# First images of the second layer: the turned block is made by VectorE in 32x32 pieces, and the transform along w runs as 64x64 tiles over four quarters of w

## The chip, the cores and the metric

The kernel runs on one core of one Trainium2 chip. The metric is the device time of one execution in microseconds (us). Three runs of the kernel before gave 2610.23, 2604.98 and 2619.08 us; their median is 2610.23 us. A difference of about 0.5% (13 us) is what a measurement of this kernel can tell from no change.

Engine names follow the profile: PE is the matmul engine (its weight loads are PEld), DVE is VectorE, ACT is ScalarE, POOL is GpSimd, SP is the engine that only issues DMAs.

## The reference, cut to what matters

The input is an image `x` of 256 x 256 pixels with 128 channels, in float32. Layer 0 is gated attention with two biases over each row. Layer 1 reads the result as 256 "tokens" (the first image axis), each an image of H = 256 rows by W = 128 pixels (the second axis by the channels), and runs a small Fourier neural operator over them. Its last part is a pair of mixing layers over groups of four tokens:

```python
h0 = instance_norm(attn, norm2_w, norm2_b)
h1 = fno_layer(h0, mix_wr[0], mix_wi[0], ..., (H, W), norm=True, act=True)
h2 = fno_layer(h1, mix_wr[1], mix_wi[1], ..., (H, W), norm=True)
out = instance_norm(h2, mon_w, mon_b) + attn

def fno_layer(x, wr, wi, bias, sw, sb, out_hw, norm=False, act=False):
    skip = jnp.einsum('bihw,oi->bohw', x, sw) + sb[:, None, None]
    xf = spectral_conv(x, wr, wi, bias, out_hw)      # FFT, 32 x 16 modes mixed, inverse FFT
    if norm: xf = instance_norm(xf)
    y = xf + skip
    return jax.nn.gelu(y, approximate=False) if act else y
```

What is changed lies between `h1` and the second layer's spectrum: `h1` is made block by block, and each block is at once transformed along w to 16 complex frequencies (32 real rows), the first half of the second layer's FFT.

## The kernel before, in words

The 256 tokens are worked on in two halves of 128, called a = 0 and a = 1, with one token on each partition. The stage in question is `first_images(a, ...)` (line 1719). It goes over 16 blocks b of a half; a block `hb[b]` holds 16 image rows by 128 pixels for all 128 tokens, 2048 numbers on each partition. Image rows are taken by their remainder j modulo 4 (`by_turn`); for row class j the four groups of 32 tokens stand in another order on the partitions (group i at i XOR j), because `skip` (line 1396) writes group i to partitions 32*(i^j).

The order of the work on PE, ACT, DVE and POOL is that of the program text (`manual_schedule`); SP's DMA issues are in program order too. Engines wait for each other only where data or buffers ask for it. One pass of the loop, at index b, issues in this order:

- `load(b+1)` and, for a = 0, `load_w(b+1)`: DMAs on SP for the modes `gs` and for `y2` (a = 1) or the old image `xw` (a = 0).
- `first_skip(b)` (16 matmuls of 32x32 into four PSUM banks `ups`) and `second_skip(b-2)` (16 more into four banks `sps`, then four `bn_stats` on DVE). For a = 1 the second one stands ahead of the first.
- `image(b)` (line 1386): 16 matmuls of 32x128 that add the inverse transform along w into the same four `ups` banks.
- `gelu` of row classes 0 and 1 on ACT (line 1821), from the `ups` banks into `hb[b]`.
- `along_w(b-2)` (line 1799): four matmuls with 128 contraction rows and 32 output rows, 512 columns each, into one bank `psA`; one ACT copy to `yA` (line 1806); one DMA to DRAM, `Yd`, on POOL's queue (line 1807). Its place in ACT's order is between the two pairs of `gelu`.
- `gelu` of row classes 2 and 3.
- `turn_back(b-1)` (line 1769): 16 PE transposes of 128x128 through four PSUM banks `htps`, and four copies to `hT` (line 1788 on DVE; row class 0 by line 1779, on DVE for a = 0 and on ACT for a = 1). The reversed views in these copies put the tokens back into their order.
- For a = 0 `add_w(b+1)` (line 1746): ACT scales (line 1754), POOL adds (line 1757) and issues the DMA to the output (line 1758), for those half blocks that were not done earlier.

The `sps`, `psA` and `htps` banks come from one ring of four; `ups` from another ring of four. For a = 1 the pass is followed by a step of `output_0`, which makes the final output of half 0: 16 matmuls and an `image` into banks `h2ps` of the `ups` ring, evacuated by ACT (line 2141) and DVE (line 2139), then two accumulating DMAs on POOL's queue (line 2163). `Yd` is read back by `second_modes` (a = 0, line 1892) and by `LastModes` (a = 1, lines 1972 and 1977), which transform along h.

Of the kernel before, what the change touches and what calls it, by code (L numbers as in the profile page):

```python
# [10 lines left out]
FP = mybir.dt.float32  # L11
# [7 lines left out]
P = 128  # L19
# [681 lines left out]
def layer1(tc, I, C, ident, x1d, upool, U, Q2, groups, out):  # L701
# [6 lines left out]
    nc = tc.nc  # L708
    NT, H, W = 256, 256, 128
    L = lambda n: I["L1_conv_" + n]  # L710
    with ExitStack() as ctx:
# [667 lines left out]
        def by_turn(t):  # L1379

            return t.rearrange("p (n j w) -> p j n w", j=4, w=W)

        def rows_of(ps):
            return ps.rearrange("p (n w) -> p n w", w=W)

# [51 lines left out]

        sp = sp3
        hstat = sp.tile([P, 64, 6], FP, name="hstat")
        ystat = sp.tile([P, 2, 64, 6], FP, name="ystat")  # L1440
        with tc.tile_pool(name="psb", bufs=4, space=PSUM) as psa:

            ps = psa.tile([P, 512], FP, tag="a", name="chps")
# [44 lines left out]
        for a in range(2):  # L1488
            h = Half()
            halves.append(h)  # L1490
            h.col = sp.tile([P, 16], FP, name=f"col_{a}")
            h.turn = sp.tile([P, 8], FP, name=f"turn_{a}")
            h.bl0 = sp.tile([P, P], FP, name=f"bl0_{a}")
            h.sums, h.summed = False, set()
            h.Gd1 = dram.tile([32, 4, 64, P], FP, name=f"Gd1_{a}")
            h.Gd2 = dram.tile([32, 4, 64, P], FP, name=f"Gd2_{a}")
            h.Yd = dram.tile([H, 32, P], FP, name=f"Yd_{a}")

        def y_blocks(a, psum, lo, hi, also=None):

            tt = slice(a * P, (a + 1) * P)
            gs = {}

            def load(u):
                if (a, u) not in xts:
                    xts[a, u] = load_x1(a, u)
                if u % 2 == 0:
                    gs[u // 2] = xp.tile([P, 4, P], FP, tag="gs", name=f"gs_{a}_{u}", bufs=3)
                    load_modes(gs[u // 2], Gd0, u // 2, tt)

            load(lo)
            load(lo + 1)
            yield 0.0
            for u in range(lo, hi):
                b, s = u // 2, u % 2
                if u + 2 < hi:
                    load(u + 2)
                xt = xts.pop((a, u))
                ps = [psum.pool.tile([P, 512], FP, tag=psum.tag, name=f"yps_{a}_{u}_{j}") for j in range(4)]
                ps = [z[:, 0:256] for z in ps]  # L1520
                for j in range(4):
                    for sc in range(2):
                        nc.tensor.matmul(  # L1523
                            rows_of(ps[j]), mpT[:, sc, tt], by_turn(xt[:, sc])[:, j],
                            start=(sc == 0), stop=False,
                        )
                    if j < 3:
                        yield 0.86
                image(ps, gs[b], bsy, range(2 * s, 2 * s + 2))
                if a == 0:  # L1530
                    yt = blocks[:, b, s * HB : (s + 1) * HB]
                else:
                    yt = xp.tile([P, HB], FP, tag="yt", name=f"yt_{u}")
                for j in range(4):
                    nc.vector.tensor_tensor(by_turn(yt)[:, j], rows_of(ps[j]), bc(rwb, 1, 2), ALU.mult)  # L1535
                for g in range(2):
                    nc.vector.bn_stats(ystat[:, a, 2 * u + g, :], yt[:, g * 512 : (g + 1) * 512])
                if a:
                    nc.gpsimd.dma_start(ydv[:, a, u * HB : (u + 1) * HB], yt)  # L1539
                if also:  # L1540
                    also(u, xt)
                yield 1.62
# [99 lines left out]
        def first_modes(a, wp, mk, psum, gts):  # L1642
# [6 lines left out]
            )  # L1649
            dg = mk("m", [P, 2, P], f"dg3_{a}")  # L1650
            ym, yv, ra, lam, r2, rho, sig = (h.col[:, k : k + 1] for k in range(7))
            nc.vector.bn_aggr(h.col[:, 0:2], ystat[:, a].rearrange("p k s -> p (k s)"))
            yield 1.0
            rsqrt(nc, wp, ra, yv, EPS, "rq")
            nc.vector.tensor_mul(lam, ra, an[:, 0:1])
# [63 lines left out]
        def first_images(a, wp, yp, psk, pst, first=None, modes=()):  # L1719
# [44 lines left out]
            if a == 0:  # L1764
                load_w(0)
                add_w(0)
            hTs = {}

            def turn_back(b):

                turned = by_turn(hb[b])
                hT = hTs[b] = {}
                for j in (1, 2, 3, 0):
                    ps = pst.tile(f"htps_{a}_{b}_{j}")
                    for n in range(4):
                        nc.tensor.transpose(ps[:, n * P : (n + 1) * P], turned[:, j, n, :], ident)  # L1776
                    t = hT[j] = wp.tile([P, 512], FP, tag="hT", name=f"hT_{a}_{b}_{j}", bufs=4)
                    if j == 0:
                        (nc.scalar.copy if a else nc.vector.tensor_copy)(t, ps)
                        continue  # L1780
                    v = t.rearrange("p (n c d x) -> p n c d x", n=4, c=2, d=2)
                    if j == 1:
                        v = v[:, :, :, ::-1].rearrange("p n c d x -> p (n c) d x")
                    elif j == 2:
                        v = t.rearrange("p (n c x) -> p n c x", n=4, c=2)[:, :, ::-1]
                    else:
                        v = t.rearrange("p (n c x) -> p n c x", n=4, c=4)[:, :, ::-1]
                    nc.vector.tensor_copy(
                        v, ps.rearrange("p (m c x) -> p m c x", m=v.shape[1], c=v.shape[2])
                    )  # L1790

            def second_skip(b):

# [4 lines left out]

            def along_w(b):

                hT = hTs.pop(b)
                psA = pst.tile(f"psA_{a}_{b}")
                for j in (1, 2, 3, 0):
                    nc.tensor.matmul(psA[32 * j : 32 * j + 32, :], bfwd, hT[j], start=True, stop=True)  # L1804
                yA = wp.tile([P, 512], FP, tag="yA", name=f"yA_{a}_{b}")
                nc.scalar.copy(yA, psA)
                (nc.scalar if a and b == 15 else nc.gpsimd).dma_start(
                    h.Yd[16 * b : 16 * b + 16].rearrange("(n j) f t -> (j f) n t", j=4),
                    yA.rearrange("f (n t) -> f n t", n=4),
                )  # L1810

            def first_skip(b):
# [68 lines left out]
        def second_modes(a, wp, mk, psum, gts, yts):  # L1881
# [5 lines left out]
            def load(c, hcs=(0, 1)):  # L1887
                yp, tag, bufs = yts[c]
                if c not in YT:
                    YT[c] = yp.tile([P, 2, 2, 512], FP, tag=tag, name=f"YT_{a}_{c}", bufs=bufs)  # L1890
                for hc in hcs:
                    nc.sync.dma_start(
                        YT[c][:, hc],
                        h.Yd[P * hc : P * hc + P].rearrange("h (r f) t -> h r (f t)", r=2)[
                            :, :, 4 * c * P : 4 * (c + 1) * P
                        ],
                    )

            def forward(c):
                ps = psum.tile(f"f1ps_{a}_{c}")  # L1900
                for r in range(2):
                    for hc in range(2):
                        for k in range(2):
                            for f in range(4):
                                nc.tensor.matmul(
                                    ps[32 * f : 32 * f + 32, r * P : (r + 1) * P],
                                    efwd[:, hc, (2 if r else 1) if k else 0, :],
                                    YT[c][:, hc, 1 - r if k else r, f * P : (f + 1) * P],
                                    start=(hc == 0 and k == 0), stop=(hc == 1 and k == 1),
                                )  # L1910
                nc.vector.tensor_copy(F[:, c].rearrange("p r t -> p (r t)"), ps[:, 0:256])
# [48 lines left out]
        class LastModes:  # L1960
# [5 lines left out]
            def load(self):  # L1966

                tile = lambda tag, bufs, n, name: xp.tile([P, 2, n], FP, tag=tag, name=name, bufs=bufs)
                rows = halves[1].Yd.rearrange("h (r f) t -> h r (f t)", r=2)
                self.low = [tile("xt", 3, 1024, f"YT0_{k}") for k in range(2)]  # L1970
                for k in range(2):
                    nc.sync.dma_start(self.low[k], rows[0:P, :, 1024 * k : 1024 * k + 1024])
                self.high = [tile("yt", 2, 512, f"YT1_{k}") for k in range(2)] + [tile("xt", 3, 1024, "YT1_2")]
                at = (slice(0, 512), slice(512, 1024), slice(1024, 2048))
                for lo, hi in ((0, 96), (96, P)):
                    for t, c in zip(self.high, at):
                        nc.sync.dma_start(t[lo:hi], rows[P + lo : P + hi, :, c])

            def spectrum(self, c, hc, r, f):
                if hc == 0:  # L1980
                    t, c = self.low[c // 2], c % 2
                else:
                    t, c = self.high[min(c, 2)], c % 2 if c > 1 else 0
                return t[:, r, 512 * c + f * P : 512 * c + (f + 1) * P]

            def synth(self, c, banks, gt, engines):

# [304 lines left out]
def constants():  # L2292
    H, W = 256, 128
    N = H * W
# [89 lines left out]
    c["efwd"] = trig.reshape(3, 32, 2, 128).transpose(3, 2, 0, 1)  # L2384
    tw = 2 * np.pi * np.outer(np.arange(16), w) / W
    bw = np.stack([np.cos(tw), -np.sin(tw)])
    c["bfwd"] = bw.reshape(32, W).T / N
    bs = bw * np.where(np.arange(16) == 0, 1, 2)[None, :, None]
    c["bsyn"] = np.tile(bs.reshape(32, W), (4, 1))
    c["atmean"] = np.where(np.arange(128) % 32 == 16, -1, 0)[:, None]  # L2390
# [63 lines left out]
```

## Time and profile before

| what | value |
|---|---|
| median of three runs | 2610.23 us |
| the profiled execution | 2606.34 us, span 2604.6 us |
| mean granted PE clock | 0.955 of full |
| busy over the span | PE 92%, PEld 60%, DVE 77%, ACT 54%, POOL 57% |
| first PE instruction on `psA`, half 0 and half 1 | 1969.9 and 2262.1 us |
| last one of half 1 | 2405.4 us |
| PE transposes `htps` | 512 instructions, 273 ns each (median) |
| PE matmuls `psA` | 256 instructions, 617 ns each (median) |
| DMA `Yd` on POOL's queue | 31 of 256 KB, 7.4 us from issue to landing (median) |

Every float32 matmul is two instructions in the trace; a PE transpose is one. Times on PE overlap: tiles in different corners of the array run side by side, so the busy time of a group is shorter than its count times its mean. Layer 0's attention scores alone (line 395) run until 1417 us. The stage of this change runs from about 1956 to 2087 us for half 0 and from about 2240 to 2409 us for half 1.

### The profile page before, as it was taken

The numbers are of one execution on the slowest core, as the hardware profiler recorded it, in microseconds if no ns is written. First come the engines' busy times: TensorE is split into PE (matmuls) and PEld (weight loads), VectorE is DVE, ScalarE is ACT, GpSimd is POOL, SyncE is SP. The second block draws the span as 40 slices with busy tenths as digits, with TensorE's granted clock in tenths as the row PEclk, the third lists the DMA queues.
The fourth block names the chain that finished last, engine by engine and source line by source line (L and its number), as shares of the span: only waits on it lengthen the run. The fifth ranks groups of instructions, "written<-read, shape, count | busy, mean of one in ns | idle before, by whom it ended". The sixth has DMA issues, their size and how long they took to land. (4 is left out here: it accounts for less than half of the span.)

```text
span 2604.6 us, 88676 instructions
## 1 busy us (share of the span) xinstructions
PE 2395.0 (92%) x37598; PEld 1555.3 (60%) x37598; DVE 2013.6 (77%) x2876; ACT 1399.0 (54%) x2700; POOL 1485.0 (57%) x1043
## 2 busy tenths in 40 slices
PE   7899999999999999999999899998989988899754
PEld 6555655656566556565655567787665565555633
DVE  7799999999999999999999457566655645355455
ACT  0377888888888888888887222000015501344232
POOL 1299999999999999999998003001136512221011
PEclk9999999999999999999999999999999998899855
DMA  9755565656566566565663110887897773899699
GB/s 367 219 100 104 103 107 104 105 106 108 103 107 106 102 108 106 104 108 103 108 105 72 25 59 11 266 274 260 309 336 253 268 251 112 228 285 254 205 388 343
DMA packets 1014245, 441.71 MB, mean 170 GB/s; under 512 B 830806, under 2 KB 946473, under 8 KB 1009496
## 3 DMA queue, kind: packets, MB, share of 16 engines
q1 hardware_dynamic: 977816, 347.93, 53.8%
q0 software_dynamic: 22832, 81.54, 9.8%
q10 hardware_dynamic: 13200, 6.56, 0.9%
q8 instruction: 298, 4.88, 0.8%
q14 instruction: 99, 0.81, 0.1%
HBM read 300.59 MB, written 135.27 MB: 167 GB/s over the span
## 5 line engine op out<-in xcount | busy, mean ns | idle before, releaser
L422 POOL TENSOR_TENSOR e<-e,b1T 128x1024 f32<-128x1024 f32 x255 | 604.4, 2370 | 84.5 <-ACT e L404 83.9
L427 POOL TENSOR_TENSOR es<-e 128x512 f32<-128x512 f32 x512 | 647.4, 1286 | 0.1
L449 DVE RECIPROCAL av<-av 128x256 f32<-128x256 f32 x256 | 452.2, 1766 | 9.1
L404 ACT ACTIVATE sc<-sc,b2T 128x512 f32<-128x512 f32 x514 | 340.0, 662 | 122.5 <-PE sc L395 109.9
L404 ACT ACTIVATE e<-sc,b2T 128x512 f32<-128x512 f32 x510 | 323.4, 694 | 0.0
L420 DVE TENSOR_TENSOR e<-sc,b1T 128x1024 f32<-128x1024 f32 x257 | 312.2, 1215 | 7.0 <-ACT sc L404 3.6
L395 PE MATMUL sc<-qkT 32*128 32x256 f32 x4096 | 294.8, 401 | 1.2 <-DVE e L420 1.2
L437 PE MATMUL av<-e,v 128*32 128x256 f32 x4096 | 268.7, 379 | 1.8 <-DVE gate L450 1.7
L1523 PE MATMUL yps<-xt,mpT 128*128 128x256 f32 x1024 | 246.3, 391 | 25.6 <-DVE yt L1535 12.8
L395 PEld LDWEIGHTS sc<-qkT 32*128 32x128 f32 x4096 | 185.7, 184 | 113.4 <-issue 52.7
L1523 PEld LDWEIGHTS yps<-xt,mpT 128*128 128x128 f32 x1024 | 191.6, 193 | 70.8 <-DVE yt L1535 22.9
L437 PEld LDWEIGHTS av<-e,v 128*32 128x32 f32 x4096 | 130.1, 109 | 125.9 <-issue 38.5
L1539 POOL DMA_DIRECT2D yd<-yt x32 | 17.4, 545 | 319.2 <-DVE yt L1535 319.2
L367 ACT ACTIVATE qkT<-qk,qb 128x512 f32<-128x512 f32 x256 | 174.4, 681 | 3.2 <-PE qk L337 3.0
L337 PE MATMUL qk<-turned,wT_wk 128*32 128x256 f32 x2048 | 164.5, 393 | 0.4 <-DVE g_ve L35 0.4
L494 ACT ACTIVATE turned<-turned 128x256 f32<-128x256 f32 x256 | 104.4, 408 | 111.7 <-DVE x1b L462 109.3
L337 PEld LDWEIGHTS u<-adft,x 128*32 128x32 f32 x4096 | 118.5, 110 | 74.9 <-issue 74.7
L442 PE MATMUL av<-es,ones 128*32 128x256 f32 x2048 | 160.7, 379 | 1.6 <-POOL es L427 1.6
L345 DVE STREAM_TRANSPOSE turned<-xk 128x1024 f32<-128x1024 f32 x128 | 157.9, 1234 | 0.4 <-DMA xk<-in_L_conv_kv_x_dram 0.2
L337 PE MATMUL qk<-turned,wn_wq 128*32 128x256 f32 x2048 | 157.9, 380 | 0.0
L1821 ACT ACTIVATE blocks<-ups,turn 128x512 f32<-128x512 f32 x128 | 92.7, 783 | 107.5 <-PE ups L1391 107.5
L337 PE MATMUL u<-adft,x 128*32 128x129 f32 x4096 | 137.0, 273 | 0.0
(577 smaller groups left out, 4146.7 us busy)
## 6 DMA issues: line engine op xcount, KB each, us to landing
xt<-x1d SPq DMA_DIRECT2D x128, 512.0 KB, 6.1
U<-in_x_dram SPq DMA_DIRECT2D x32, 1024.0 KB, 10.3
xk<-in_x_dram SPq DMA_DIRECT2D x512, 64.0 KB, 3.2
xk<-in_L_conv_kv_x_dram SPq DMA_DIRECT2D x512, 64.0 KB, 2.7
x1d<-x1b SPq DMA_DIRECT2D x512, 64.0 KB, 2.2
out_dram<-w POOLq DMA_DIRECT2D x64, 512.0 KB, 7.2
x<-x1d SPq DMA_DIRECT2D x126, 256.0 KB, 3.3
y<-yd SPq DMA_DIRECT2D x62, 512.0 KB, 8.8
```

The costliest lines, as they stand in the source:

```text
L337: nc.tensor.matmul(out[hd], w[:, hd], src, start=start, stop=stop)
L345: nc.vector.transpose(turned[:, a : b + 1 : b - a].rearrange("p k (b c) -> p k b c", c=32), t)
L367: nc.scalar.activation(r["qkT"], ps, AF.Identity, bias=self.qb)
L395: nc.tensor.matmul(sc[h // 2][:, h % 2, c * 256 : (c + 1) * 256], qkT[p, 256 + c * P : 256 + (c + 1) * P], qkT[p, 0:256], start=True, stop ...
L404: nc.scalar.activation(r["e"][1][:, :, c, :] if hp and s < NS - 1 else z, z, AF.Exp, bias=b2T[:, c, s : s + 1])
L420: nc.vector.tensor_tensor(e, sc.rearrange("p h x -> p (h x)"), w, ALU.mult)
L422: nc.gpsimd.tensor_tensor(e, e, w, ALU.mult)
L427: nc.gpsimd.tensor_tensor(es, e[:, :, 0, :], e[:, :, 1, :], ALU.add)
L437: nc.tensor.matmul(ps[hd, 0:256], p["v"][:, 2 * (s % 2) + c, hd], r["e"][h // 2][:, h % 2, c, :], start=(c == 0), stop=(c == 1),)
L442: nc.tensor.matmul(ps[32 * h : 32 * h + 32, 256:512], self.ones, r["es"][h // 2][:, h % 2, :], start=True, stop=True,)
L449: nc.vector.reciprocal(rd, rd)
L1523: nc.tensor.matmul(rows_of(ps[j]), mpT[:, sc, tt], by_turn(xt[:, sc])[:, j], start=(sc == 0), stop=False,)
```

## The change

`turn_back` no longer uses PE and PSUM. Two DVE transposes per block, each of 1024 numbers on each partition, turn every 32x32 piece in place of the 128x128 transposes. After them a partition holds one pixel of a quarter of w for a group of 32 tokens, so `along_w` has to add up four quarters of w, and it does so for two token groups at once: 16 matmuls of 64 contraction rows, 64 output rows and 256 columns, in four tiles of 64x64, four in a row added up in each tile. Half of each weight block is zero; its non-zero places (g XOR j) put the token groups back into order. The result lies in two banks, is copied by two ACT instructions of 256 columns each, and goes to DRAM in another layout, in runs of 64 numbers where there were runs of 128. The readers of `Yd` follow that layout. `turn_back`'s buffer is one tile of 2048 numbers in place of four of 512. `ystat` is shared by the two halves, and the constant `bfwd` grows from 128 x 32 to 128 x 512 numbers. The loop's order of calls is as before; with the PE transposes gone, `along_w` is the last work on PE in a pass.

```diff
-        ystat = sp.tile([P, 2, 64, 6], FP, name="ystat")
+        ystat = sp.tile([P, 64, 6], FP, name="ystat")
...
-            h.Yd = dram.tile([H, 32, P], FP, name=f"Yd_{a}")
+            h.Yd = dram.tile([H, 2, 2, 16, 64], FP, name=f"Yd_{a}")
...
-            hTs = {}
+            turned = {}
 
             def turn_back(b):
 
-                turned = by_turn(hb[b])
-                hT = hTs[b] = {}
-                for j in (1, 2, 3, 0):
-                    ps = pst.tile(f"htps_{a}_{b}_{j}")
-                    for n in range(4):
-                        nc.tensor.transpose(ps[:, n * P : (n + 1) * P], turned[:, j, n, :], ident)
-                    t = hT[j] = wp.tile([P, 512], FP, tag="hT", name=f"hT_{a}_{b}_{j}", bufs=4)
-                    if j == 0:
-                        (nc.scalar.copy if a else nc.vector.tensor_copy)(t, ps)
-                        continue
...
-                    nc.vector.tensor_copy(
-                        v, ps.rearrange("p (m c x) -> p m c x", m=v.shape[1], c=v.shape[2])
-                    )
+                T = turned[b] = wp.tile([P, 8, 8, 32], FP, tag="hT", name=f"hT_{a}_{b}", bufs=1)
+                src = hb[b].rearrange("p (n k l x) -> p k n l x", k=2, l=8, x=32)
+                for k in range(2):
+                    nc.vector.transpose(T[:, :, k::2].rearrange("p l n x -> p n l x"), src[:, k])
...
             def along_w(b):
 
-                hT = hTs.pop(b)
-                psA = pst.tile(f"psA_{a}_{b}")
-                for j in (1, 2, 3, 0):
-                    nc.tensor.matmul(psA[32 * j : 32 * j + 32, :], bfwd, hT[j], start=True, stop=True)
-                yA = wp.tile([P, 512], FP, tag="yA", name=f"yA_{a}_{b}")
-                nc.scalar.copy(yA, psA)
+                T = turned.pop(b)
+                ps = [pst.tile(f"psA_{a}_{b}_{r}") for r in range(2)]
+                for c in range(4):
+                    for j in range(2):
+                        for r in range(2):
+                            q, o = slice(64 * r, 64 * r + 64), slice(64 * j, 64 * j + 64)
+                            nc.tensor.matmul(
+                                ps[r][o, 0:256], bfwd[q, j, c], T[q, 4 * j + c],
+                                start=(c == 0), stop=(c == 3),
+                            )
+                yA = wp.tile([P, 4, 4, 32], FP, tag="yA", name=f"yA_{a}_{b}")
+                for r in range(2):
+                    nc.scalar.copy(
+                        yA[:, :, 1:3] if r else yA[:, :, 0::3],
+                        ps[r][:, 0:256].rearrange("p (n k x) -> p n k x", k=2, x=32),
+                    )
                 (nc.scalar if a and b == 15 else nc.gpsimd).dma_start(
-                    h.Yd[16 * b : 16 * b + 16].rearrange("(n j) f t -> (j f) n t", j=4),
-                    yA.rearrange("f (n t) -> f n t", n=4),
+                    h.Yd.rearrange("(k l) r g f x -> (l r g f) k x", l=2)[:, 8 * b : 8 * b + 8],
+                    yA.rearrange("p n (k h) x -> p (n k) (h x)", k=2),
                 )
...
+        def by_token(t):
+
+            return t.rearrange("p (g f h x) -> p f h g x", g=2, h=2, x=32)
...
                     nc.sync.dma_start(
-                        YT[c][:, hc],
-                        h.Yd[P * hc : P * hc + P].rearrange("h (r f) t -> h r (f t)", r=2)[
-                            :, :, 4 * c * P : 4 * (c + 1) * P
-                        ],
+                        YT[c][:, hc].rearrange("p r (g f x) -> p r g f x", g=2, x=64),
+                        h.Yd[P * hc : P * hc + P, :, :, 4 * c : 4 * c + 4],
                     )
...
-                                    YT[c][:, hc, 1 - r if k else r, f * P : (f + 1) * P],
+                                    by_token(YT[c][:, hc, 1 - r if k else r])[:, f],
...
-    c["bfwd"] = bw.reshape(32, W).T / N
+    fw = np.zeros((2, 2, 32, 2, 4, 2, 2, 16))
+    for g in range(2):
+        for j in range(2):
+            fw[:, g, :, j, :, :, g ^ j] = (bw.reshape(2, 16, 4, 32) / N).transpose(3, 2, 0, 1)
+    c["bfwd"] = fw.reshape(128, 2, 4, 64)
```

More of the change, by code (lines that the diff above doesn't have):

```diff
@@ L1536, in y_blocks @@
                 for g in range(2):
-                    nc.vector.bn_stats(ystat[:, a, 2 * u + g, :], yt[:, g * 512 : (g + 1) * 512])
+                    nc.vector.bn_stats(ystat[:, 2 * u + g, :], yt[:, g * 512 : (g + 1) * 512])
                 if a:
@@ L1651, in first_modes @@
             ym, yv, ra, lam, r2, rho, sig = (h.col[:, k : k + 1] for k in range(7))
-            nc.vector.bn_aggr(h.col[:, 0:2], ystat[:, a].rearrange("p k s -> p (k s)"))
+            nc.vector.bn_aggr(h.col[:, 0:2], ystat.rearrange("p k s -> p (k s)"))
             yield 1.0
@@ L1766, in first_images @@
                 add_w(0)
-            hTs = {}
+            turned = {}
             def turn_back(b):
-                turned = by_turn(hb[b])
-                hT = hTs[b] = {}
-                for j in (1, 2, 3, 0):
-                    ps = pst.tile(f"htps_{a}_{b}_{j}")
-                    for n in range(4):
-                        nc.tensor.transpose(ps[:, n * P : (n + 1) * P], turned[:, j, n, :], ident)
-                    t = hT[j] = wp.tile([P, 512], FP, tag="hT", name=f"hT_{a}_{b}_{j}", bufs=4)
-                    if j == 0:
-                        (nc.scalar.copy if a else nc.vector.tensor_copy)(t, ps)
-                        continue
[L1781 to L1788, printed above, removed]
-                        v, ps.rearrange("p (m c x) -> p m c x", m=v.shape[1], c=v.shape[2])
-                    )
+                T = turned[b] = wp.tile([P, 8, 8, 32], FP, tag="hT", name=f"hT_{a}_{b}", bufs=1)
+                src = hb[b].rearrange("p (n k l x) -> p k n l x", k=2, l=8, x=32)
+                for k in range(2):
+                    nc.vector.transpose(T[:, :, k::2].rearrange("p l n x -> p n l x"), src[:, k])
             def second_skip(b):
@@ L1968, in load @@
                 tile = lambda tag, bufs, n, name: xp.tile([P, 2, n], FP, tag=tag, name=name, bufs=bufs)
-                rows = halves[1].Yd.rearrange("h (r f) t -> h r (f t)", r=2)
+                rows = halves[1].Yd
+                part = lambda t: t.rearrange("p r (g f x) -> p r g f x", g=2, x=64)
                 self.low = [tile("xt", 3, 1024, f"YT0_{k}") for k in range(2)]
                 for k in range(2):
-                    nc.sync.dma_start(self.low[k], rows[0:P, :, 1024 * k : 1024 * k + 1024])
+                    nc.sync.dma_start(part(self.low[k]), rows[0:P, :, :, 8 * k : 8 * k + 8])
                 self.high = [tile("yt", 2, 512, f"YT1_{k}") for k in range(2)] + [tile("xt", 3, 1024, "YT1_2")]
-                at = (slice(0, 512), slice(512, 1024), slice(1024, 2048))
+                at = (slice(0, 4), slice(4, 8), slice(8, 16))
                 for lo, hi in ((0, 96), (96, P)):
                     for t, c in zip(self.high, at):
-                        nc.sync.dma_start(t[lo:hi], rows[P + lo : P + hi, :, c])
+                        nc.sync.dma_start(part(t[lo:hi]), rows[P + lo : P + hi, :, :, c])
             def spectrum(self, c, hc, r, f):
@@ L1983, in spectrum @@
                     t, c = self.high[min(c, 2)], c % 2 if c > 1 else 0
-                return t[:, r, 512 * c + f * P : 512 * c + (f + 1) * P]
+                return by_token(t[:, r])[:, 4 * c + f]
             def synth(self, c, banks, gt, engines):
```

## The prediction, made before the changed kernel ran

> **What bounds the kernel now.** I first laid the stage into stretches, then read single passes in order of time, then the waits, and last the rows that price the new work. The stretches (columns: length; busy time of PE, PEld, DVE, ACT, POOL with counts; clock; DMA share; GB/s):
>
> ```profile
> 1969.87:2027.27 57.40, 53.72 (x844) 33.07 (x841) 34.17 (x55) 35.45 (x47) 43.38 (x33) 0.94 0.86 285
> 2027.27:2060.45 33.18, 33.18 (x605) 19.83 (x601) 25.34 (x42) 22.59 (x31) 15.58 (x13) 1.00 0.67 214
> 2262.00:2345.00 83.00, 77.58 (x1715) 45.75 (x1717) 46.51 (x72) 41.86 (x64) 20.17 (x24) 1.00 1.05 286
> ```
>
> PE looks like the bound: 33.18 of 33.18 us in the middle of half 0, 77.58 of 83 in half 1. That speaks for taking transposes off PE. But busy is no proof that PE sets the pace, so I read one pass of half 0:
>
> ```profile
> 2033.87 1.06 PE L1804 MATMUL psA<-hT,k_bfwd 128*32 128x512 f32 x8
> 2033.95 1.45 ACT L1821 ACTIVATE blocks<-ups,turn 128x512 f32<-128x512 f32 x2 [3.32 <-PE ups L1391]
> 2034.86 1.97 PE L1776 MATMUL htps<-ident,blocks 128*128 128x128 f32 x16
> 2035.29 0.58 ACT L1806 COPY yA<-psA 128x512 f32<-128x512 f32 x1
> 2035.56 1.89 DVE L1788 COPY hT<-htps 128x512 f32<-128x512 f32 x3 [0.72 <-PE htps L1776]
> 2035.76 1.47 ACT L1821 ACTIVATE blocks<-ups,turn 128x512 f32<-128x512 f32 x2
> ...
> 2036.76 1.15 PE L1406 MATMUL ups<-blocks,bl 32*32 32x512 f32 x28
> 2037.28 0.13 PEld L1406 LDWEIGHTS ups<-blocks,bl 32*32 32x32 f32 x5 [0.32 <-ACT blocks L1821]
> ...
> 2039.36 1.17 PE L1391 MATMUL ups<-k_bsyn,gs 32*128 32x128 f32 x32
> ```
>
> The line at 2037.28 decides. Row class 3 of `first_skip` needs the bank that the fourth `gelu` empties; it ended at 2035.76 + 1.47 = 2037.23. So the pass is a ring: image ends, two `gelu`, the `yA` copy, two `gelu`, `first_skip`'s last class, `second_skip`, image (2037.23 to 2039.36 is 2.13), 6.6 us in all. PE's transposes fit into the time that ACT needs anyway, with 0.3 us to spare. Half 1 has the same ring through `h2ps`:
>
> ```profile
> 2303.34 1.06 PE L1804 MATMUL psA<-hT,k_bfwd 128*32 128x512 f32 x8
> ...
> 2306.23 1.58 PE L1406 MATMUL h2ps<-blocks,bl 32*32 32x512 f32 x32
> ...
> 2306.75 0.15 PEld L1406 LDWEIGHTS h2ps<-blocks,bl 32*32 32x32 f32 x8 [0.32 <-ACT blocks L1821]
> 2307.74 1.17 PE L1391 MATMUL h2ps<-k_bsyn,gs 32*128 32x128 f32 x32
> ```
>
> and the table of waits has it 13 times there:
>
> ```profile
> PEld h2ps L1406 <- ACT blocks L1821: 5.0, 13, 0.8
> ```
>
> In the other passes of half 0 (successive `psA` starts 7.3 to 10.5 us apart against 6.6) POOL works nearly without a pause on `add_w` and `Yd`, and SP's loads wait for it. Rows that price the new work:
>
> ```profile
> L345 DVE STREAM_TRANSPOSE turned<-xk 128x1024 f32<-128x1024 f32 x128 | 157.9, 1234 | 0.4 <-DMA xk<-in_L_conv_kv_x_dram 0.2
> L508 ACT COPY U<-u 128x258 f32<-128x258 f32 x1 | 0.4, 423 | 0.0
> L1807 POOL DMA_DIRECT2D Yd<-yA x31 | 24.0, 773 | 77.3 <-ACT yA L1806 58.9 <-ACT blocks L1821 15.7 <-DVE hT L1788 2.7
> L1539 POOL DMA_DIRECT2D yd<-yt x32 | 17.4, 545 | 319.2 <-DVE yt L1535 319.2
> ```
>
> **The transposes leave PE.** Per block 16 PE transposes (1.97 us) and four copies of 0.68 (0.60 on ACT) go. By the ring above they hide behind ACT, so on the path this removes nothing: at most the PE order gets 1.9 us shorter where ACT does not wait. On DVE two transposes of 1.23 us, 2.47 us, take the place of three or four copies, 2.0 to 2.7 us. They are free to start only when `along_w(b-2)` has read the single buffer; behind them on DVE stand `output_0`'s two evacuations (half 1) or the next `bn_stats` (half 0). They would end 4.4 us after image's end; the evacuations are due at about 6 us, the `bn_stats` at 5.7. So zero, and if the new view cost double (2.4 us each), some 1 us per pass.
>
> **`along_w` gets longer on PE.** Now four tiles each take two instructions of 512 columns: 1.06 us. New: four tiles each take eight of 256 columns, 2048 columns against 1024. The slope per column comes from median durations, 273 ns at 128, 379 at 256, 592 at 512 columns: 0.83 ns. So 1.70 us, plus what a group of eight rounds costs beyond its columns: image, eight rounds of 128 columns, 1.17 - 0.85 = 0.32. I take 1.95 us, 1.77 to 2.1. No row has a 64-row tile; 32-row tiles (image, skips) and 64-column tiles run side by side in this trace, so I exclude a serial run (some 3.5 us). The Trainium skill's TensorEngine Tiling (Array Packing), section Instruction Overhead, speaks against many short matmuls: about 60 cycles for each. For the six extra rounds against today's two it would make some 0.15 us as an estimate, where today's 1.06 in two rounds against image's 1.17 in eight, both over 1024 columns a tile, shows 0.11.
>
> **ACT gets the wait.** Counted from the first `gelu`, the second pair starts now at 1.81 us. New: `psA` ends at -0.08 + 1.95 = 1.87, hand-over 0.07 (at 2365.83 to 2365.90 `yA` waited for `psA`), then two copies of 256 columns at 0.42 less the 0.11 by which neighbours on ACT overlap, 0.62: 2.56. The second pair of `gelu`, and with it row class 3 of the next skip, comes 0.75 us later. With `psA` at 1.77 it is 0.57; with unoverlapped copies 0.97. Nothing else in the ring gets shorter.
>
> **Where this counts.** Half 1 has 14 passes with `psA`: 10.5 us. But they take 10.34 us on average, while the cleanest with `output_0` takes 9.36 (2364.77 to 2374.13); the rest is stalls on issue and on `gs`, which run by time, so part of a later chain falls into them. I take off a third: 7.0. Half 0 has six passes at the ring's pace (6.6 to 6.75 apart): 4.5.
>
> **POOL's queue.** `Yd` goes from 512 runs of 512 B to 1024 of 256 B. Issue time: 0.545 for 128 runs, 0.773 for 512, so 0.59 ns a run and +0.3 us for each `Yd`. In half 0 POOL sets the pace in about eight passes: 2.4 us; elsewhere POOL idles before `Yd`. Bounds: 0 and 0.77 (doubled).
>
> **`Yd`'s landing.** ACT's queue, mean packet 497 B, shows 28 ns a packet (13200 packets, 0.9% of 16 engines); layer 0's loads, mean 152 B, 14 ns. So a 256 B run costs 14 to 28, and a `Yd` 64 runs per DMA engine, 0.9 to 1.8 us against 0.9. I take 0.3 once at each half's end. The Trainium skill, DMA: Bandwidth & Descriptors, section Specifications, says that below 512 B a transfer falls off line rate through read-modify-write; doubled per byte it would give, as an estimate, +0.9 at each end, and the sum 1.2 more.
>
> **The drain of half 1.** Block 15 waits twice: `along_w(14)` starts at 2401.28 and ends at 2403.23, DVE's transposes end at 2405.65, `psA` at 2407.6, the copies at 2408.4. Today `yA` ends at 2406.65: +1.75.
>
> **Nothing:** `bfwd` (256 KB in place of 16) is issued at 1529 us and first read at 1970; without that cover about 3 us. `YT` in 1 KB runs is loaded under half 1's blocks. `ystat` is read by DVE before half 1 writes it.
>
> **Sum:** 7.0 + 4.5 + 2.4 + 0.6 + 1.75 = 16.2 us. The profiled run, 2606.3, would become 2622.5; it lies 3.9 below the median of the runs, 2610.2, and from that the forecast is 2626.
>
> **Rivals.** *PE sets the pace after all* (the other side). If the 0.32 us waits are a reading of modelled ends, each pass is PE's own work: 1.06 + 1.97 go, 1.95 comes, -1.1 us in 14 + 6 passes, -22 us: 2588. It decides from the point where the second pair of `gelu` starts no later than 1.81 us after the first. For: PE's 100% in the middle stretch. Against: 13 waits on ACT, none of them needed if PE were late. *The stalls take it up:* half 1's passes stay at 10.3 us, as DMA share 1.05 suggests, and only half 0 and the drain count: some +6, 2616. Against: passes of 9.4 us stand between the longer ones. *The buffers bite:* the single turned tile, a slower DVE transpose or a longer landing (`yA` has two buffers, and its copy waits up to 6.5 us for an earlier `Yd` at the end of half 0) add another 1 us to 20 passes: 2645.
>
> **Chances.** Forecast 0.50, PE 0.17, stalls 0.17, buffers 0.16. About 0.5%, 13 us, is what a measurement of this kernel can tell from no change. The forecast's own range, +9 to +24, lies below that line with 0.10; the PE case is faster; the stalls case is the same but for 0.02. So faster 0.17, same 0.25, slower 0.58. The range 2600 to 2646 leaves out most of the PE case and the worst of the buffers, 0.2.
>
> **What would show it.** Right: `psA` about 1.95 us; ACT's `yA` waiting about 0.5 us for `psA` in every pass; PE idle, instead of transposing, before the skip's last class, with longer waits on ACT; half 0's middle passes at 7.3 us; `Yd` issues of about 1.07 us. Wrong: middle passes of 5.5 us, or a `psA` under 1.5 us; `output_0` or `bn_stats` waiting for DVE's transposes would speak for the buffers.

## The result, and the profile after

The changed kernel has a median of 2623.14 us (2614.38 to 2630.59, 20 runs) against 2607.64 (2600.00 to 2624.36, 20 runs) for the kernel before. The ratio is 1.0042, with a 95% interval of 1.0028 to 1.0055: about 11 us slower (7 to 14). The quotient of the two medians alone would be 1.0059; I go by the ratio and its interval. The sign of the forecast holds and the median lies 3 us from the forecast 2626, but the cost by the ratio, 11 us, is smaller than the 16 that I had summed, and its interval crosses the 0.5% line of 13 us. By that line of the prediction it counts as no change, to which it gave 0.25, and not as slower, to which it gave 0.58. The terms of the sum fared less well than the sum.

The profiled execution of the changed kernel took 2614.38 us, with a span of 2612.3 at a mean granted clock of 0.955, as before. Its span is 7.7 us longer. From the first `gelu` of a half to the end of its last `yA` copy, half 0 took 126.1 us before and 124.0 after; half 1 took 164.8 before and 176.0 after. So in this pair of profiles half 1 carries more than all of it.

The stretch of half 1 that I showed of before (length; busy time of PE, PEld, DVE, ACT, POOL with counts; clock; DMA share; GB/s):

```profile
2262.00:2345.00 83.00, 74.37 (x1700) 38.41 (x1696) 47.66 (x62) 35.65 (x58) 20.24 (x23) 1.00 1.01 260
```

PE is busy less (77.58 before), DVE about as much, and the core moved less in the same time (286 GB/s before). PE got its relief and the stage got slower. One pass of half 0, in order of time, shows why:

```profile
2027.57 1.96 PE L1795 MATMUL psA<-hT,k_bfwd 64*64 64x256 f32 x32
2027.66 1.45 ACT L1819 ACTIVATE blocks<-ups,turn 128x512 f32<-128x512 f32 x2 [3.32 <-PE ups L1395]
2029.62 0.65 ACT L1801 COPY yA<-psA 128x256 f32<-128x256 f32 x2 [0.52 <-ACT blocks L1819]
2029.68 2.37 DVE L1778 STREAM_TRANSPOSE hT<-blocks 128x1024 f32<-128x1024 f32 x2 [1.61 <-ACT blocks L1819]
2030.15 1.46 ACT L1819 ACTIVATE blocks<-ups,turn 128x512 f32<-128x512 f32 x2
...
2031.67 0.13 PEld L1410 LDWEIGHTS ups<-blocks,bl 32*32 32x32 f32 x5 [0.52 <-ACT blocks L1819]
2033.75 1.17 PE L1395 MATMUL ups<-k_bsyn,gs 32*128 32x128 f32 x32
2034.85 0.45 PE L1795 MATMUL psA<-hT,k_bfwd 64*64 64x256 f32 x4
```

`psA` takes 1.96 us where it took 1.06. ACT's first two `gelu` end at 2029.11, and ACT then idles 0.5 us until `psA` is done at 2029.53. (The bracket names the instruction that came last by the record's modelled ends, ACT's own `gelu`; what the copy needs is `psA`.) The second pair of `gelu` starts 2.49 us after the first, where it was 1.81, and the next `psA` starts at 2034.85, 7.28 after this one, where it was 6.6. The waits tell the same, first in half 0 and then in half 1 (total us, times, longest):

```profile
PEld ups L1410 <- ACT blocks L1819: 27.8, 36, 1.4
ACT yA L1801 <- PE psA L1795: 8.9, 12, 3.7
```

```profile
PEld h2ps L1410 <- ACT blocks L1819: 28.0, 37, 1.4
```

Before, the wait of `ups` in the same stretch of half 0 (1966 to 2080 us) was 4.2 us in 14 waits, and that of `h2ps` in half 1 was 5.0 us in 13. PE now waits for `gelu` in the place where it transposed. The rows that price the new work, from the groups of instructions by shape (busy time, mean ns of one, idle time before and what ended it):

```profile
L1778 DVE STREAM_TRANSPOSE hT<-blocks 128x1024 f32<-128x1024 f32 x64 | 75.9, 1223 | 76.0 <-ACT blocks L1819 62.3 <-issue 11.1 <-ACT yA L1801 2.7
L1805 POOL DMA_DIRECT2D Yd<-yA x31 | 28.4, 917 | 85.2 <-ACT yA L1801 80.8 <-ACT blocks L1819 4.5
```

The transposes cost 1.22 us each, as in layer 0. The `Yd` issue rose by 0.14 us to 0.92, half of the 0.3 that I had taken. Last, the end of half 1 in order of time:

```profile
2399.28 1.95 PE L1795 MATMUL psA<-hT,k_bfwd 64*64 64x256 f32 x30 [0.64 <-issue]
2401.36 2.37 DVE L1778 STREAM_TRANSPOSE hT<-blocks 128x1024 f32<-128x1024 f32 x2 [3.35 <-issue]
2403.66 2.45 DVE L1785 BATCH_NORM_STATS2 hstat<-sps 128x6 f32<-128x512 f32 x4
2404.37 2.55 PE L1795 MATMUL psA<-hT,k_bfwd 64*64 64x256 f32 x32 [1.30 <-DVE hstat L1785]
2407.06 2.37 DVE L1778 STREAM_TRANSPOSE hT<-blocks 128x1024 f32<-128x1024 f32 x2 [0.95 <-issue]
2409.58 1.96 PE L1795 MATMUL psA<-hT,k_bfwd 64*64 64x256 f32 x32 [2.66 <-DVE hT L1778]
```

And the last two `psA` of the kernel before; the one ahead of them started at 2396.51:

```profile
2401.28 1.06 PE L1804 MATMUL psA<-hT,k_bfwd 128*32 128x512 f32 x8
2404.17 1.85 PE L1804 MATMUL psA<-hT,k_bfwd 128*32 128x512 f32 x8
```

With little other work left, the blocks 13, 14 and 15 run nearly in series through the single turned buffer. The transposes of block 14 start at 2401.36, when `psA` of block 13 has read the buffer (2399.28 + 1.95 = 2401.23). Behind them on DVE stand the `bn_stats` of the last skip, and `psA` of block 14 waits for the bank that the first of these empties. Then PE waits 2.66 us for the transposes of block 15. The last two `psA` start 6.37 and 5.21 us after the one before (the first of them at 2398.00); before the change these were 4.78 and 2.89.

### The profile page after: what moved, and what is told of

Its sections match the earlier page's. It is cut to its first block, busy times and chain, and to the rows that moved or that the text cites. A ratio compares the mean times of both kernels' runs of the same rounds, so it can differ in the third digit from the quotient of the medians.

```text
span 2612.3 us, 89105 instructions
## 1 busy us (share of the span) xinstructions
PE 2388.0 (91%) x37854; PEld 1528.2 (58%) x37854; DVE 2018.1 (77%) x2828; ACT 1394.3 (53%) x2716; POOL 1490.1 (57%) x1043
```

## The experiments

The theory: a pass is the ring through ACT, and the change lengthens it by the time that `yA` waits for `psA`. The rivals: PE sets the pace; other stalls set it and the ring does not matter; something else in the change (the `Yd` runs, the single buffer) costs the time.

**Half the work of `along_w`**: `psA` becomes short again, and all else of the change stays.

```diff
-                for c in range(4):
+                for c in range(2):
...
-                                start=(c == 0), stop=(c == 3),
+                                start=(c == 0), stop=(c == 1),
```

> The changed kernel with two of the four quarters of w added up: half the matmuls of along_w are left out, psA takes about 1.1 us instead of 1.96. Theory: yA no longer waits for psA, the second pair of gelu starts about 1.86 us after the first instead of 2.49; half 0's middle passes go from 7.25 to about 6.65 us, and half 1's clean ones from 10.28 to about 9.65 with the mean held at about 10.4 by the DMA engines; the drain is some 1.5 us shorter. Total about 2614 us, -9 from the changed kernel. Rival (the two copies on ACT cost, not the wait): middle passes of 7.1 us or more.

Measured: 2609.46 us, ratio to the kernel before 0.9997 (0.9972 to 1.0021). The pass of half 0 in the order of time:

```profile
2033.16 1.09 PE L1795 MATMUL psA<-hT,k_bfwd 64*64 64x256 f32 x16
2033.25 1.45 ACT L1819 ACTIVATE blocks<-ups,turn 128x512 f32<-128x512 f32 x2 [3.32 <-PE ups L1395]
2034.59 0.64 ACT L1801 COPY yA<-psA 128x256 f32<-128x256 f32 x2
2035.11 1.48 ACT L1819 ACTIVATE blocks<-ups,turn 128x512 f32<-128x512 f32 x2
```

The second pair starts 1.86 us after the first, the middle passes of half 0 take 6.66, and the loss is gone. DVE's transposes, the `Yd` runs and the two copies were all still there. So the length of `psA` is the change's cost, within the 0.2 to 0.3% of the interval. Halving `along_w` also takes work off PE, so this run alone can't tell ACT's wait from PE's own time; the next one can.

**The copy after all four `gelu`**, in the changed kernel and in the kernel before: the ring no longer holds `psA` at all.

```diff
                     gelu(b, ps, (0, 1))
+                    gelu(b, ps, (2, 3))
                 if b > 1:
                     along_w(b - 2)
-                if b < 16:
-                    gelu(b, ps, (2, 3))
```

> The changed kernel with along_w called after all four gelu of a pass, so that on ACT the two yA copies come behind the second pair of gelu; the order on PE stays. Theory (ACT's ring): the second pair of gelu starts 1.34 us after the first instead of 2.49, and half 1's clean passes go from 10.28 to about 8.9 us; half 1 from its first gelu to its last yA copy falls from 176 to about 160 us, the whole to about 2605 us (-18 from the changed kernel, a little under the kernel before). In half 0 the second skip may wait up to 0.5 us for the psA banks. Rival (PE's order sets the pace): the order on PE is as it was, so passes stay at 10.28 us and the time at 2623 us.

> The kernel before with the same reorder: along_w after all four gelu. Theory: ACT's ring is only 0.3 us longer than PE's own work in the kernel before, so half 1's clean passes go from 9.36 to about 9.0 us and no further, -4 us in all, about 2603 us. Rival (ACT does not matter): 2608 us, passes of 9.36 us.

Measured: the changed kernel 2617.01 us, 1.0022 (0.9998 to 1.0047); the kernel before 2612.91, 1.0021 (1.0003 to 1.0038). The ring shortened as it should: the middle passes of half 0 take 6.11 us, and 6.40 in the kernel before. PE's own work is the same in them, so in half 0 it is ACT's order that sets these passes. But half 1 did not follow, and both kernels miss the times that I had expected, 2605 and 2603 us. In the changed kernel its passes take some 11.05 us on average, against the 8.9 expected, and half 1 lasts 180.0 us, no shorter than without the edit: there two profiles show 176.0 and 183.2 (the second in the run without POOL's additions below, whose half 1 is that of the changed kernel). So in half 1 something else stands next in line.

**The `yA` copy on DVE**, in both kernels, takes it out of ACT's order:

```diff
-                    nc.scalar.copy(
+                    nc.vector.tensor_copy(
```

> The changed kernel with the two yA copies on DVE ahead of its transposes instead of on ACT. Theory: ACT runs four gelu in a row, half 1's clean passes are about 8.9 us as in the run with the copies last, without its wait for the psA banks; DVE's two copies (0.4 us each) and two transposes end about 5.1 us after image's end, ahead of output_0's evacuations at about 5.4, so DVE may add 0.2 us. About 2603 to 2607 us. Rival (DVE's transposes are late once ACT is not): passes of 9.5 us or more, the evacuations waiting on DVE, 2612 us or more.

> The kernel before with its one yA copy on DVE instead of ACT; PE transposes stay. Theory: with ACT out of the way PE's own work is the bound, half 1's clean passes about 9.0 us (PE relieved of transposes would be 8.9), some -4 us, about 2603 us: the change's lighter PE is worth 0.1 to 0.2 us a pass at most once the copy is off ACT. Rival (PE relief is worth 1.1 us a pass once ACT is free): this kernel is 10 us or more slower than the changed kernel with its copies on DVE.

Measured: 2618.92 us, 1.0034 (1.0015 to 1.0052), and 2611.79, 1.0013 (0.9990 to 1.0036). The same picture: 6.26 and 6.36 us in the middle of half 0, about 11.2 and 11.05 in half 1. These times miss the 2603 to 2607 us that I had expected as well. A shorter ring gains in half 0's middle passes and nothing in half 1, with the change or without.

**The second bound of half 1.** In half 1 `output_0`'s DMAs add to what lies in memory. These three kernels write without adding: the kernel before, the changed one, and the changed one with the copy last.

```diff
-                    nc.gpsimd.dma_start(outv[:, 0, px], t[:, s * HB : (s + 1) * HB], accum_op=ALU.add)
+                    nc.gpsimd.dma_start(outv[:, 0, px], t[:, s * HB : (s + 1) * HB])
```

> The kernel before with output_0's DMAs writing plainly instead of accumulating, so half 0 of the output holds only its last term. In the list of DMA packets of half 1 an accumulating 4 KB packet takes 327 ns and a plain one 159, and all packets together fill the 16 DMA engines: about 10.3 us of each for a pass. Theory (two bounds in half 1, ACT's ring and the DMA engines): without accumulation a pass needs 7.6 us of DMA, and half 1 falls to the ring's 9.4 us a pass from 10.34; half 1 from first gelu to last yA copy 153 us from 165, the whole about 12 us less. Rival (the stalls between passes are PE's own, instruction fetch): passes stay at 10.3 us.

> The changed kernel with the same plain writes (half 0 of the output holds only its last term). Theory: half 1's passes are ACT's ring alone, 10.28 us each; half 1 about 166 us from 176, and 0.92 us a pass, 13 us in all, plus 3 for the drain longer than in the kernel before with plain writes. Rival (the change's cost in half 1 is DMA, its runs of 256 B): without the DMA bound the two kernels' passes differ by less than 0.3 us.

> The changed kernel with along_w after all four gelu and with plain writes (half 0 of the output holds only its last term). Theory: with both bounds off, passes of about 8.9 us, half 1 about 147 us, some 6 us under the kernel before with plain writes. Rival (the shorter ring gained little because its order of work is itself worse, not for the DMA): passes stay at 10 us or more.

Measured: 2592.40 us, 0.9932 (0.9901 to 0.9962); 2602.51, 0.9972 (0.9956 to 0.9988); 2586.99, 0.9919 (0.9891 to 0.9948). Here is the DMA queue that POOL feeds, over 134 us of half 1, in the kernel before and in its form without additions (packets, MB, share of 16 engines):

```profile
q0 software_dynamic: 4540, 16.17, 55.2%
```

```profile
q0 software_dynamic: 4837, 17.24, 32.3%
```

More bytes take 32.3% of the engines in place of 55.2%: a 4 KB packet that adds took 327 ns (median), a plain one 159. With the other queue's 45.8% that is 101% in the kernel before: its DMA engines were full in this stage (no slice of 10 us of this execution shows more than 106%), with as much work as its passes are long, some 10.4 us. With plain writes they are not, and the ring stands alone. Half 1 in the three kernels, in the order above (columns as before):

```profile
2262.00:2376.00 114.00, 114.00 (x2552) 68.16 (x2560) 68.47 (x107) 61.29 (x95) 20.88 (x34) 1.00 0.88 295
```

```profile
2262.00:2376.00 114.00, 108.46 (x2436) 56.52 (x2440) 69.01 (x88) 53.20 (x88) 21.66 (x32) 1.00 0.85 277
```

```profile
2262.00:2376.00 114.00, 111.54 (x2736) 61.93 (x2748) 78.21 (x99) 58.73 (x100) 23.57 (x35) 1.00 0.92 312
```

The passes take 9.65, 10.28 and 9.11 us. In the first kernel half 1 is 12 us shorter, as expected; the whole is some 18 us shorter (10 to 26). The change adds 0.63 to a pass, and the last two `psA` come at 6.46 and 5.21 us where they came at 4.77 and 2.89. So 13 × 0.63 + 4.0 = 12.2 us; half 1 grew from 152.8 to 165.2, 12.5. The third kernel shows that the ring could give 1.2 us a pass back if the DMA engines had room: its half 1 lasts 152.7 (147 were expected). The first line also settles the rival that PE sets the pace: PE is busy for 114.00 of 114 us, and taking 16 transposes a block away from it makes the pass longer, while keeping ACT from waiting makes it shorter.

**Half 0 without POOL's additions**, in the kernel before and the changed one:

```diff
-                    nc.gpsimd.tensor_tensor(t[:, px], t[:, px], ys.pop((b, s)), ALU.add)
+                    ys.pop((b, s))
```

> The kernel before without POOL's additions in add_w, so the old image is missing from 21 half blocks of half 0's output; its loads, ACT's scaling and the DMAs stay. Theory (POOL's chain sets half 0, and a slower ring falls into it): half 0's passes go down to the ring's 6.6 us, first psA to last from 109.1 to about 98 us. Rival (half 0 is held by the loads on SP's queue, not by POOL): passes of 7.5 us and more stay.

> The changed kernel without the same additions (the old image is missing from 21 half blocks). Theory: passes of 7.25 us throughout half 0, first psA to last about 105 us, so that the 0.65 us a pass, 8 us in all, that POOL's chain covers in the full kernels comes to light beside the kernel before without additions. Rival: the two kernels' half 0 stay within 2 us of each other, as with the additions.

Measured: 2597.73 us, 0.9951 (0.9927 to 0.9976), and 2616.93, 1.0019 (1.0001 to 1.0037). Half 0 in the changed kernel, then in these two (kernel before, changed):

```profile
1972.00:2060.00 88.00, 82.00 (x1501) 39.17 (x1490) 57.16 (x72) 57.97 (x89) 59.78 (x46) 1.00 0.83 275
```

```profile
1972.00:2060.00 88.00, 88.00 (x1606) 52.28 (x1602) 66.07 (x107) 63.88 (x88) 20.04 (x32) 1.00 0.87 312
```

```profile
1972.00:2060.00 88.00, 82.91 (x1559) 38.56 (x1559) 59.45 (x74) 59.96 (x92) 20.08 (x29) 1.00 0.86 290
```

POOL falls from 59.8 to 20 busy us, and all passes now go at the ring's pace: 6.59 to 6.66 us, and 7.24 to 7.28 with the change. Half 0 lasts 108.5 and 119.0. So without POOL's chain the change costs 10.5 us in half 0; with it, the profiled pair shows none. The times go the same way: the two ratios lie some 18 us apart, where the full kernels lie 11 apart, though the intervals overlap. So most of what the ring loses in half 0 lies under `add_w`.

**`Yd` in long runs**: 128 runs of 2 KB in the changed kernel.

```diff
-                    h.Yd.rearrange("(k l) r g f x -> (l r g f) k x", l=2)[:, 8 * b : 8 * b + 8],
-                    yA.rearrange("p n (k h) x -> p (n k) (h x)", k=2),
+                    h.Yd[16 * b : 16 * b + 16].rearrange("h r g f x -> (h r g f x)").rearrange("(p y) -> p y", p=P),
+                    yA.rearrange("p n k x -> p (n k x)"),
```

> The changed kernel with Yd written in 128 runs of 2 KB, in an order that its readers do not expect, so that the second layer's spectrum is of permuted numbers. Theory: the 256 B runs cost POOL 0.37 us of issue for each Yd (0.91 to 0.55) and the DMA engines hardly anything; 0 to 2 us of the whole. Rival (the small runs are the cost): 8 us or more come back, and half 1's passes shorten by 0.5 us.

Measured: 2616.72 us, 1.0015 (0.9998 to 1.0032). Its middle passes (7.24 us) are those of the changed kernel, and its half 1, 181.7 us, lies between the 176.0 and 183.2 of that kernel's half 1. By the ratios it is 7 us below the changed kernel, with intervals that just overlap, where I had expected 0 to 2; the profile shows no place for a gain. So a part of some 7 us for the short runs stays open. The kernel with two quarters kept them and still had the time of the kernel before, to within 0.3%.

**The image loads of `output_0` on POOL's queue**, with the copy last, since SP's queue was where the copy-last kernel showed a new wait:

```diff
...
-                load_modes(got[b], halves[0].Gd2, b)
+                load_modes(got[b], halves[0].Gd2, b, queue=nc.gpsimd)
```

> The changed kernel with along_w after all four gelu, and with output_0's four loads of modes in each pass issued on POOL's queue instead of SP's; accumulation stays. With the copies last, half 1's ring is 9.1 us (seen with plain writes), yet its passes take 11 us on average, and SP's mode loads wait 51.7 us for earlier y loads to land. Theory A (the DMA engines are full: share 0.98): the move changes nothing, passes stay at about 11 us, 2617 us. Theory B (SP's queue, ten loads in order in each pass with a limited number in flight, is the bound): six loads a pass instead of ten, passes of about 9.5 us, half 1 about 155 us from 180, some 2595 us.

Measured: 2608.29 us, 0.9997 (0.9982 to 1.0012). SP's queue, what it waited for in half 1 (total us, times, longest), in the changed kernel, with the copy last, and with this edit:

```profile
SPq L1419 <- DMA y<-yd: 18.6, 6, 4.7
```

```profile
SPq L1419 <- DMA y<-yd: 51.7, 20, 4.9
```

```profile
SPq L1735 <- PE ups L1410: 74.1, 12, 8.6
...
SPq L1735 <- DMA y<-yd: 9.1, 6, 2.1
```

The wait of the image loads behind `y` is nearly gone (0.7 us), half 1 falls from 180.0 to 170.3 us, and its passes average 10.46, with the DMA engines' share at 1.01. That lies between the two expectations: by the profile SP's queue was part of what held the copy-last kernel, and with it gone the pass stands near the DMA engines' 10.4. In the times this edit by itself is not clear of noise (1.0022 to 0.9997, with intervals that overlap); the two edits together repair the changed kernel's loss (1.0042 to 0.9997) but do not beat the kernel before.

## Why the prediction was right, and where its steps were not

**The ring: right.** `psA` 1.96 us (said 1.95), the copies 0.65 (0.62), the second pair of `gelu` 2.49 after the first (2.56), the middle passes of half 0 7.24 to 7.28 (7.3). Halving `along_w` brings 6.66 back, and moving the copy gives 6.11.

**Transposes off PE at nothing, and onto DVE at nothing: right** for the passes, by the same runs; in the drain DVE's transposes do count. The rival that PE sets the pace fell. The Trainium skill's Perfetto Trace Analysis, section Optimization Strategies, advises to keep the matmul engine highly utilized and, where it idles, to optimize the engines that block it; its second half agrees with these runs, but utilization alone misled here: 114.00 busy us at 9.65 a pass, 111.54 at 9.11.

**Half 1, 7.0 us: right in size in the profiled pair, by two errors that cancel.** The mean pass grew from 10.34 to 10.92, 0.58 in 13 intervals, 7.5 us. I had taken 0.75 a pass and off it a third that the stalls would absorb. With plain writes the step is 0.63 (9.65 to 10.28): the second pair of `gelu` comes 2.50 us after the first there, not 2.56, and the 9.36 that I had read as the cleanest pass was shorter than the undisturbed ring, because it followed a late one. And almost nothing was absorbed: the mean grew by nearly all of the step. Why it did is not shown. With additions the passes before already took the 10.4 us of the DMA engines, and a ring of 10.28 would fit into that. In the kernel before, the passes ran from 8.74 to 12.00 us; in the changed one all but one of the 13 take 10.28 or more, so late passes are hardly ever followed by short ones. The size, too, is that of one pair: in the pair without POOL's additions, whose half 1 is the same, the mean pass grew from 10.49 to 11.44, 12 us.

**Half 0, 4.5 us for the ring and 2.4 for POOL's issues: the step that failed, as far as the profiles tell.** The profiled half 0 got 2 us shorter. The pair with plain writes, whose half 0 is the same code, got 5 us longer (123.4 to 128.3). The three kernels with the copy last share one half 0 and show 120.8 to 124.8, so single profiles spread by 4 us, and the two pairs together give some 1.4 us. I had counted each pass at the ring's pace as lost time, and took the passes that POOL paces as fixed. They are not: without the additions of `add_w` the same ring costs 10.5 us, so their chain covers most of that. The first seven passes, which held most of it, took 57.4 us before and 53.7 after, and 56.0 and 56.3 in the other pair, with a slower ring. The price of an issue was also half of what I took, 0.14 us.

**The drain of half 1, 1.75 us: mis-sized, 3.9 in the profiles** (4.78 + 2.89 against 6.37 + 5.21), 4.0 with plain writes. I had let `along_w(14)` start when it started before the change and made only block 15 wait. The single buffer holds block 14 too, by way of DVE: the transposes wait for the buffer, the `bn_stats` wait behind the transposes, and `psA` waits for the bank that they empty.

**Landing, 0.6 us: not seen.** The median from issue to landing of `Yd` was 7.4 us before and is 7.0. The Trainium skill's DMA: Bandwidth & Descriptors, section Specifications, has transfers below 512 B lose line rate; no trace here shows the doubling that the prediction estimated from it for 256 B runs, and the times of the kernel with long runs leave a smaller loss open.

The sum that the profiles support: 13 × 0.58 + 3.9 = 11.4 us in half 1, and -2 to +5 in half 0, against 11 by the ratio. So the mechanism, a longer wait of `yA` in ACT's order, held, but that the median came within 3 us of 2626 is partly luck: half 0 was put too high, the drain too low, and the quotient of the medians lies above the ratio.

**Open.** The end of half 0 varies between single profiles: the last two `yA` copies idled 5.3 to 6.5 us for an earlier `Yd` before the change and in the changed kernel with plain writes. In the changed kernel itself only the last one did: it started at 2078.90 after 6.70 idle us, 0.1 us after that `Yd` had landed. From the first to the last `yA` copy, half 0 took 113.0 us before and 110.3 after, but 110.3 and 114.6 in the pair with plain writes: its share is somewhere between -3 and +4. Why passes with a shorter ring average 11 us in half 1, more than the 10.4 of full DMA engines, is explained only in part by SP's queue. Two turned buffers, which should remove most of the drain's 4 us, were not tried.

## What to carry to other kernels

Follow one pass back from its last wait before counting a busy engine as the bound: PE at 100% was doing work that fitted into ACT's time. A matmul whose result is evacuated in the middle of another engine's order has a price there and not on its own engine, so place the evacuation, or price its delay, first. And shortening the ring pays only down to the next bound, here the DMA engines at some 10.4 us a pass, which adding writes had filled.

## What the runs showed of the hardware

- On the queue that POOL feeds, a 4 KB packet took 327 ns (median) with DMAs that add to memory and 159 with plain ones: without the additions, half 1 of the kernel before shortened from 164.8 to 152.8 us.
- POOL's time to issue a `Yd` or `yd` DMA was 0.545 us for 128 runs, 0.773 for 512 and 0.92 for 1024: the price of a further run falls from 0.59 to 0.28 ns. `Yd` in 128 runs of 2 KB took 0.558.
- The 32 matmuls of 64x64 f32 tiles over 256 columns that make one `psA` in the trace took 1.96 us together, 16 of them 1.09, at a granted clock of 1.00.
- SP issued later loads only once earlier ones had landed: 51.7 us over 20 waits behind `y` in half 1 of the copy-last kernel, whose loads of `y` landed after 8.0 us there (median) against 5.0 in the changed kernel. What makes it wait, no run shows.
